# The C rows of a selective scan: a matmul from the small projection tile in place of a repeating transfer and a ScalarE copy

## The chip, the cores and the metric

The kernel runs on one core of a Trainium2 chip. The core has five engines with queues of their own: TensorE (PE in the profile; its weight loads are PEld), VectorE (DVE), ScalarE (ACT), GpSimd (POOL) and SyncE (SP), which here issues the DMA transfers; 16 DMA engines carry these. Each engine takes its instructions in the order of the program and waits for the others by semaphores. SBUF is the working memory of 128 partitions, PSUM the memory that TensorE writes, in banks of 512 fp32 numbers a partition.

The metric is the device time of one execution in microseconds (us), as the median over runs.

## What is computed

The program is a sequence of four layers on images of 4 x 64 x 64 positions and 128 channels. The first two hold a selective scan in four directions over the 4096 positions (`D` is 128 channels in layer 0 and 256 in layer 1, `N` is 16 states, the rank `R` is 4 and 8). Cut to what matters here:

```python
x_dbl = jnp.einsum('bkdl,kcd->bkcl', xs, x_proj_w)       # R + 16 + 16 rows a direction
dts, Bs, Cs = jnp.split(x_dbl, [R, R + N], axis=2)
dts = jnp.einsum('bkrl,kdr->bkdl', dts, dt_w)
delta = jax.nn.softplus(dts + dt_b[None, :, :, None])

def step(h, t):
    x_t, d_t, B_t, C_t = t
    h = jnp.exp(d_t[..., None] * A) * h + (d_t * x_t)[..., None] * B_t[:, :, None, :]
    return (h, jnp.einsum('bkdn,bkn->bkd', h, C_t))
```

Around the scans stand projections, small convolutions and normalisations; layers 2 and 3 (a message-passing layer and neighbourhood attention) follow after the scans.

## The kernel before

**Tiling.** A *task* is the scan of one image over 128 channels: 4 tasks in layer 0, 8 in layer 1 (two tiles of channels an image; the second task of such a pair has `t.first` set and uses the first one's projection again). A task has 16 *steps*: 4 directions times 4 stretches of `TS` = 1024 positions. A step has 16 *units* of 8 channels: the 128 partitions of a unit are 16 states times 8 channels. So there are 12 x 16 x 16 = 3072 units and 192 steps.

**One unit.** `load` (L429, SP's queue) brings `dub`, the product of delta and x for 8 channels, repeated for 16 states, from DRAM. `times_b` (L436, GpSimd) multiplies it by `repB`, the B rows, into `h`. `decay` puts delta, spread over the partitions, into PSUM by two bf16 matmuls (`da`, L444) and takes the exponent in place on ScalarE (L446). `scan` runs the recurrence on VectorE (L455), and after each odd unit multiplies the pair of `h` by C, `hc` (L465). `save` copies the last column of the pair as `state` (L476, ScalarE). `add_up` sums `hc` over the states by TensorE into `yps` (L536), `keep` (L546) and `sum_so_far` (L511, L519) carry the running sum. `h` has buffers for three pairs, `da` two, `dub` five.

**The order** is written out by hand in `Scans.run`: in slot u it issues the scan of u, the product with B of u + 3, C if u opens a step, the state of the last pair, the decay of u + 2, the summing of the last pair, then *pieces*: of the preparation of a later step, and of side work (the projections, convolutions and outputs of other images), and last the load of u + 6. A planner (`Plan`) keeps an account in us of how far TensorE, ScalarE and GpSimd are behind; `plan.slot` adds what a slot holds of fixed work (its two last arguments are TensorE's sums and ScalarE's copies) and a piece is let in when it fits. DMAs of the pieces are posted with a due time and issued in a later slot.

**The preparation** of a step (`prepare`) begins 22 units ahead of it. TensorE projects the 1024 positions in two halves of 512, side by side: rows 0 to R + 31 of the small tile `xd` hold delta's R rows, B's 16 and C's 16 of the first half, rows 64 on those of the second. ScalarE copies it from PSUM into `xd` (one buffer), and it is stored as `xdd` in DRAM (L348). The second task of a pair reads delta's R rows back (L356). From `xdd`, two transfers (L363) repeat each of the 16 rows of B and of C for 8 partitions into `repB` (two buffers) and `repC` (one buffer), 512 KB each. From `xd`'s first R rows, TensorE (`ms<-xd`), ScalarE and GpSimd make delta, its three bf16 parts and its product with x, which goes to DRAM (`dud`, L394) to be read as `dub`.

**C** is read by VectorE from PSUM: `bring_c`, at the first unit of a step, copies `repC` into the tile `C` (two banks, one buffer) on ScalarE (L482). It stands in ScalarE's queue behind the exponent of unit 1 and the pieces of the slot before, and ahead of the state copy, the exponent of unit 2 and the copy of `y`.

Operations that the planner counts all bear the line of its helper, L97.

Of the kernel before, what the change touches and what calls it, by code (L numbers as in the profile page):

```python
# [9 lines left out]
F32 = mybir.dt.float32  # L10
# [7 lines left out]
P = 128  # L18
H = 64
HW = 64  # L20
L = HW * HW
T = 512
NCH = L // T
ROWS = T // HW
NS = 16
ND = 4
NG = 16
TS = 1024
HALVES = TS // T
# [15 lines left out]
class Consts:  # L45


    def __init__(self, tc, pool, d_gather, d_spread):
        nc = tc.nc

        gather = pool.tile([P, 56], F32, name="gather")
        nc.sync.dma_start(out=gather, in_=d_gather)
        self.gather = [gather[:, 24 - 8 * jj : 56 - 8 * jj] for jj in range(4)]

        self.spread = pool.tile([96, 4, P], BF16, name="spread")
        with tc.tile_pool(name="spread32", bufs=1) as tmp:
            spread = tmp.tile([96, 4, P], F32, name="spread32")
            nc.sync.dma_start(out=spread, in_=d_spread)
            nc.vector.tensor_copy(self.spread, spread)
        self.ident = pool.tile([P, P], F32, name="ident")  # L60
        make_identity(nc, self.ident)
        self.ones128 = pool.tile([P, P], F32, name="ones128")
        nc.vector.memset(self.ones128, 1.0 / 128.0)
        self.cen128 = pool.tile([P, P], F32, name="cen128")
        nc.vector.tensor_sub(self.cen128, self.ident, self.ones128)
        self.cen256 = pool.tile([P, P], F32, name="cen256")
        self.neg256 = pool.tile([P, P], F32, name="neg256")
        nc.vector.memset(self.neg256, -1.0 / 256.0)
        nc.vector.tensor_add(self.cen256, self.ident, self.neg256)
        self.eps = pool.tile([P, 1], F32, name="eps")  # L70
        nc.vector.memset(self.eps, EPS)
# [34 lines left out]
UNIT = 3.6  # L106
# [7 lines left out]
class Plan:  # L114
# [22 lines left out]
    def post(self, chain, issue, due=0.0):  # L137

        if self.running:
            self.posted.append((chain, max(self.done, due), issue))  # L140
        else:
            issue()
# [77 lines left out]
class ScanWeights:  # L220


    def __init__(self, tc, pool, layer, d_xp, d_dtw, d_av):
        nc = tc.nc
        self.layer, self.nct, self.rank = layer, TILES[layer], RANKS[layer]
        nct, rank = self.nct, self.rank
        self.nc, self.pool, self.d_xp, self.d_dtw = nc, pool, d_xp, d_dtw
        n = ND * nct * NG
        av = pool.tile([P, n + 2 * ND * nct], F32, name=f"av{layer}")
        nc.sync.dma_start(out=av, in_=d_av)  # L230
        self.a = av[:, 0:n]
        nc.scalar.activation(self.a, self.a, AF.Exp)
        nc.vector.tensor_scalar_mul(self.a, self.a, -1.0)
        self.dtb = av[:, n : n + ND * nct].rearrange("p (k t) -> p k t", k=ND)
        ds = av[:, n + ND * nct :].rearrange("p (t k) -> p t k", t=nct)
        self.dsum = pool.tile([P, nct], F32, name=f"dsum{layer}")
        nc.vector.reduce_sum(self.dsum, ds, axis=AX.X)


    def load(self):  # L240

# [27 lines left out]
class Scans:  # L269
# [14 lines left out]
    @staticmethod  # L284
    def half(i):
        return slice(i * T, (i + 1) * T)
# [30 lines left out]
    def prepare(self, t, step):  # L317

        nc, W, half, post = self.plan, t.W, self.half, self.plan.post
        begin = self.plan.now  # L320
        k, c = t.steps[step]
        R = W.rank
        rows = R + 2 * NS
        if t.first is None:
            yield "PE" if W.nct > 1 else "PE ACT"

        xd = self.tile("xd", 1, shape=(P, T))
        if t.first is None:
            xdd = t.xdd[step] = self.dram.tile(
                [rows, TS], F32, name="xdd", tag=f"xdd{W.layer}", bufs=(4, 2 * len(t.steps))[W.layer]  # L330
            )
            ps = self.bank()
            for ti in range(W.nct):
                for i in range(HALVES):
                    nc.tensor.matmul(
                        image(ps[i * H : (i + 1) * H, :]),
                        W.xp[:, ti, k, :],
                        self.view(t.xc[ti], k, c, i, HALVES),
                        start=ti == 0,
                        stop=ti == W.nct - 1,  # L340
                    )
                if ti + 1 < W.nct:
                    yield "PE ACT" if ti + 2 == W.nct else "PE"
            nc.scalar.copy(xd, ps)

            def store_xd():
                for i in range(HALVES):
                    nc.sync.dma_start(out=xdd[:, half(i)], in_=xd[i * H : i * H + rows, :])  # L348

            post("prep", store_xd)  # L350
            ready = max(self.plan.done, self.plan.now) + LANDING
            yield "PE ACT"
        else:
            xdd, ready = t.first.xdd[step], begin
            for i in range(HALVES):
                nc.sync.dma_start(out=xd[i * H : i * H + R, :], in_=xdd[0:R, half(i)])  # L356
            yield "PE ACT", self.plan.now + LANDING
        out = t.prepared[step] = {}

        def repeat(i):  # L360
            rep = out["BC"[i]] = self.tile("rep" + "BC"[i], 2 - i)
            src = bass.AP(xdd.tensor, xdd.offset + (R + i * NS) * TS, [[TS, NS], [0, 8], [1, TS]])
            nc.sync.dma_start(out=rep, in_=src)  # L363

        for i, free in enumerate((5, 8)):
            post("rep", lambda i=i: repeat(i), max(begin + free * UNIT, ready))

        bias = W.dtb[:, k, t.ct : t.ct + 1]
        delta, low = self.tile("delta", 1), self.tile("low", 1)
        for i in range(HALVES):  # L370
            ps = self.bank()
            nc.tensor.matmul(
                ps,
                W.dtw[i * H : i * H + R, k, t.ct * P : (t.ct + 1) * P],
                xd[i * H : i * H + R, :],
                start=True,
                stop=True,
            )
            nc.scalar.activation(low[:, half(i)], ps, AF.Abs, bias=bias)
            nc.scalar.activation(delta[:, half(i)], ps, AF.Relu, bias=bias)  # L380
            yield "PE ACT" if i + 1 < HALVES else "ACT"
        nc.scalar.activation(low, low, AF.Exp, scale=-1.0)
        yield "ACT"
        nc.scalar.activation(low, low, AF.Ln, bias=1.0)
        yield "POOL"
        nc.gpsimd.tensor_add(delta, delta, low)
        yield "ACT POOL"
        parts = self.tile("parts", 1, shape=(P, 3, TS), dtype=BF16)
        nc.scalar.copy(parts[:, 0, :], delta)
        nc.gpsimd.tensor_mul(image(low), image(delta), self.view(t.xc[t.ct], k, c, 0, 1))  # L390
        yield "POOL"
        t.x_done = step == len(t.steps) - 1
        dud = out["du"] = self.dram.tile([P, TS], F32, name="dud", tag="dud", bufs=3)
        post("prep", lambda: nc.sync.dma_start(out=dud, in_=low))  # L394
        nc.gpsimd.tensor_sub(delta, delta, parts[:, 0, :])
        yield "ACT"
        nc.scalar.copy(parts[:, 1, :], delta)
        yield "POOL"
        nc.gpsimd.tensor_sub(parts[:, 2, :], delta, parts[:, 1, :])


        def own(part, j):
            if j == part == 0:
                out["delta"] = self.tile("dp", 2, shape=(96, 4, TS), dtype=BF16)
            nc.sync.dma_start(
                out=out["delta"][32 * part : 32 * part + 32, j, :], in_=parts[32 * j : 32 * j + 32, part, :]
            )

        for i in range(12):
            j, part = divmod(i, 3)  # L410
            post("rep", lambda part=part, j=j: own(part, j), begin + (9 + 0.7 * i) * UNIT)
        yield ""
# [65 lines left out]
    def bring_c(self, u):  # L478

        t, step, jj, j, g = self.unit(u)  # L480
        c = self.psum.tile([P, TS], F32, name="C", tag="C", bufs=1)
        self.nc.scalar.copy(c, t.prepared[step]["C"])  # L482
        t.prepared[step]["C"] = c

# [69 lines left out]
    def run(self, between):  # L556
# [10 lines left out]
        for u in range(-7, total):  # L567
# [14 lines left out]
            if u > 0 and u % 8 == 1:  # L582
                self.sum_so_far(u - 1)
            even, eighth, first_one = u % 2 == 0, u % 8 == 1, u % NG == 0
            self.plan.slot(
                u, 1.6 * even + 1.0 * eighth, 0.25 * even + 0.7 * (u % 8 == 0) + 1.1 * first_one
            )
            ahead, rest = divmod(u + AHEAD, NG)
            if rest == 0:
# [556 lines left out]
def scan_layers(tc, C, nb, x_in, d0, s0, d1, s1, out):  # L1146

    nc = tc.nc
    with ExitStack() as es:
# [1 line left out]
        side_pool = es.enter_context(tc.tile_pool(name="side", bufs=1))  # L1151
        psum = es.enter_context(tc.tile_pool(name="psum", bufs=1, space=PSUM))
        dram = es.enter_context(tc.tile_pool(name="dram", bufs=1, space=DRAM))
        Ws = [ScanWeights(tc, pool, i, *d) for i, d in enumerate((s0, s1))]
        plan = Plan(nc)
        side = Side(tc, C, side_pool, psum, dram, x_in, d0, d1, plan)
        side.x2 = out
# [876 lines left out]
```

## Time and profile before

| | us |
|---|---|
| median of 3 runs | 14127.82 (14112.14 to 14149.53) |
| the profiled execution, its time | 14143.9 |
| its span, first to last instruction | 14142.1 |
| scan stage, 195 to 11466 us | 11271 |
| VectorE busy in the scan stage | 10460.65 |
| GpSimd busy in the scan stage | 9272.69 |
| TensorE busy in the scan stage | 8107.24 |
| ScalarE busy in the scan stage | 6639.11 |
| mean granted TensorE clock in the scan stage | 0.70 |
| busy share of the 16 DMA engines there | 0.87, 213 GB/s |

The span's 40 equal slices show the stages: the scans fill the first 32, layers 2 and 3 the rest.

```profile
PE   5777777777766777677777777777777766657999
DVE  4998899989998999889998999999999945775666
ACT  3666566646665566556665555555555546554555
POOL 4777788768876888778887888888888843550000
DMA  6888889989898888989889888888888842442000
```

How to read the page: a group's line has the program line, the engine, the operation, the tile that is written and those that are read, the shapes and the count; then its busy time, the mean duration of one in ns, the idle time of the engine just before such instructions, and who ended most of it. In a list of waits a line has the engine and the tile that waited, whom it waited for, the sum in us, how many times, and the longest. In a timeline a line has start, length, engine, line and operation; neighbours of one kind are merged, and an fp32 matmul counts as two records.

### The profile page before, as it was taken

What the parts mean: (1) busy time and instruction counts of PE and PEld (TensorE: products, weight loads), DVE (VectorE), ACT (ScalarE), POOL (GpSimd) and SP (SyncE); (2) the same over time, 40 slices, a digit from 0 to 9 for tenths busy, and PEclk for the clock granted to TensorE, in tenths of its full rate; (3) what the DMA queues carried; (4) which work ended last, traced back from release to release, by engine and by line L of the source; (5) the groups of instructions that cost most, each with busy time, mean ns of one, the idle gap of its engine ahead of it and who ended that gap; (6) DMA issues with size and microseconds to landing.
All of it is one profiled execution on the core that took longest, in us unless ns stands there. A gap on an engine that the chain in (4) does not pass through costs nothing. (4 is left out here: it accounts for less than half of the span.)

```text
span 14142.1 us, 120207 instructions
## 1 busy us (share of the span) xinstructions
PE 10269.8 (73%) x36408; PEld 2614.3 (18%) x36408; DVE 12076.7 (85%) x6647; ACT 8107.1 (57%) x10782; POOL 9862.3 (70%) x4606
## 2 busy tenths in 40 slices
PE   5777777777766777677777777777777766657999
PEld 1111111111111111111111111111111111113555
DVE  4998899989998999889998999999999945775666
ACT  3666566646665566556665555555555546554555
POOL 4777788768876888778887888888888843550000
PEclk7766767767776767777766777767776678778999
DMA  6888889989898888989889888888888842442000
GB/s 163 218 217 220 206 216 226 219 212 217 219 232 202 213 214 213 224 208 218 219 217 223 217 204 202 204 202 222 205 208 202 196 111 65 104 109 59 13 14 8
DMA packets 900351, 2567.23 MB, mean 182 GB/s; under 512 B 145271, under 2 KB 166911, under 8 KB 891511
## 3 DMA queue, kind: packets, MB, share of 16 engines
q1 hardware_dynamic: 899703, 2559.53, 73.8%
q8 instruction: 291, 4.77, 0.2%
q14 instruction: 357, 2.92, 0.1%
HBM read 2135.67 MB, written 272.37 MB: 170 GB/s over the span
## 5 line engine op out<-in xcount | busy, mean ns | idle before, releaser
L436 POOL TENSOR_TENSOR h<-dub,repB 128x1024 f32<-128x1024 f32 x3072 | 7174.4, 2356 | 1326.2 <-DMA dub<-dud 947.5
L455 DVE TENSOR_TENSOR_SCAN h<-da,state,h 128x1024 f32<-128x1024 f32 x2304 | 5322.0, 2339 | 468.8 <-POOL h L436 267.4
L446 ACT ACTIVATE da<-da,av 128x1024 f32<-128x1024 f32 x3072 | 3339.4, 1088 | 2949.2 <-PE da L444 2938.4
L444 PE MATMUL da<-dp,spread 96*128 96x512 bf16 x6144 | 2533.8, 506 | 2516.6 <-DVE h L455 2459.6
L465 DVE TENSOR_TENSOR hc<-h,C 128x2048 f32<-128x2048 f32 x1536 | 3513.6, 2288 | 150.1 <-ACT C L482 92.0
L536 PE MATMUL yps<-hc,gather 128*32 128x512 f32 x12288 | 2473.7, 890 | 6.7 <-DVE hc L465 6.7
L455 DVE TENSOR_TENSOR_SCAN h<-da,h 128x1024 f32<-128x1024 f32 x768 | 1730.6, 2279 | 369.9 <-POOL h L436 266.3
L444 PEld LDWEIGHTS <-spread 96*128 96x128 bf16 x6144 | 565.4, 108 | 5811.1 <-issue 5664.3
L97 POOL TENSOR_TENSOR delta<-delta,low 128x1024 f32<-128x1024 f32 x192 | 451.8, 2353 | 593.5 <-ACT low L97 539.0
L97 PE MATMUL ms<-d,wts 128*128 128x512 f32 (+3 forms) x900 | 675.2, 876 | 198.7 <-POOL d L97 101.7
L97 ACT ACT_TABLE_LOAD x600 | 769.8, 1283 | 12.1 <-PE ms L97 1.7
L97 PE MATMUL ms<-xd,xpdt 8*128 8x512 f32 (+1 forms) x768 | 631.1, 913 | 127.2 <-ACT xd L97 34.9
L97 ACT CAST parts<-delta 128x1024 bf16<-128x1024 f32 x384 | 400.9, 1044 | 399.5 <-POOL delta L97 375.0
L519 PE MATMUL yps<-y,ident 128*128 128x512 f32 x576 | 515.1, 985 | 104.6 <-ACT y L546 104.0
L97 ACT ACTIVATE low<-ms,av 128x512 f32<-128x512 f32 x384 | 263.9, 687 | 525.2 <-PE ms L97 506.7
L1813 ACT ACTIVATE s<-s,nmax 128x512 f32<-128x512 f32 x512 | 366.1, 717 | 249.4 <-DVE nmax L1810 244.6
L97 POOL TENSOR_TENSOR low<-delta,xc 128x1024 f32<-128x1024 f32 x192 | 501.8, 2614 | 1.5
L97 PE MATMUL ms<-pad,diag 96*32 96x504 f32 (+1 forms) x2304 | 410.9, 818 | 94.0 <-DMA pad<-xid 48.2
L1441 ACT ACTIVATE hid<-hid,relb 128x1024 f32<-128x1024 f32 x288 | 322.7, 1146 | 262.9 <-DVE hid L1436 262.6
L536 PEld LDWEIGHTS yps<-hc,gather 128*32 128x32 f32 x12288 | 283.7, 128 | 1016.5 <-issue 1008.2
L1543 POOL TENSOR_TENSOR acc<-acc,part 128x1024 f32<-128x1024 f32 x120 | 311.2, 2599 | 215.7 <-DVE part L1537 160.3
L1802 PE MATMUL sps<-k,q 32*128 32x512 f32 x1024 | 444.4, 664 | 21.2 <-DVE s L1809 21.2
(276 smaller groups left out, 11290.2 us busy)
## 6 DMA issues: line engine op xcount, KB each, us to landing
dub<-dud SPq DMA_DIRECT2D x3072, 512.0 KB
dp<-parts SPq DMA_DIRECT2D x2304, 64.0 KB
repB<-xdd SPq DMA_DIRECT2D x192, 512.0 KB
repC<-xdd SPq DMA_DIRECT2D x192, 512.0 KB
dud<-low SPq DMA_DIRECT2D x192, 512.0 KB
spread<-gd SPq DMA_DIRECT2D x72, 1024.0 KB
pad<-xid SPq DMA_DIRECT2D x192, 256.0 KB
szd<-o SPq DMA_DIRECT2D x96, 256.0 KB
```

What stands on the lines that cost most here:

```text
L97: return call(*args, **kw)
L436: self.nc.gpsimd.tensor_mul(dbu, self.live.pop(("dub", u)), t.prepared[step]["B"])
L444: self.nc.tensor.matmul(da[:, cols], self.C.spread[:, jj, :], dp[:, j, cols], start=True, stop=True)
L446: self.nc.scalar.activation(da, da, AF.Exp, scale=t.W.a[:, at : at + 1])
L455: nc.vector.tensor_tensor_scan(h[:, way], da[:, way], h[:, way], 0.0 if step % NSTEP == 0 else t.states[step - 1][:, u % NG : u % NG + 1], ...
L465: nc.vector.tensor_mul(hc, pair, t.prepared[step]["C"].unsqueeze(1).to_broadcast([P, 2, TS]))
L519: self.nc.tensor.matmul(self.like_part(yps, k), self.C.ident, self.part(t.y, k, c, b), start=True, stop=False)
L536: self.nc.tensor.matmul(out, self.C.gather[jj], rhs, start=False, stop=jj == 3)
L1441: nc.scalar.activation(hid, hid, AF.Gelu, bias=self.relb[:, m, t : t + 1])
L1543: (nc.vector if alone and pair else nc.gpsimd).tensor_add(acc, acc, part)
L1802: nc.tensor.matmul(sps[:, h, :], q[ch, toks], k[ch, keys], start=True, stop=True)
L1813: nc.scalar.activation(s[:, i, :], s[:, i, :], AF.Exp, bias=nmax[:, h : h + 1], accum_out=total[:, h : h + 1],)
```

## The change

C no longer goes by way of `xdd` and `repC`. A selector `pick`, 128 x 128, is made at the start from the identity: column 8 n + i has a one in row R + 16 + n and another in row 64 + R + 16 + n. At the first unit of a step, two fp32 matmuls, one for each half of the positions, multiply `pick`'s rows by `xd`'s and so write C's 16 rows, each repeated for 8 partitions, into the two banks of `C`. For this `xd` is kept until then and has two buffers, and the second task of a pair reads all rows of `xdd` back. The transfer of `repC`, its tile and the copy L482 go. The planner's account of a step's first unit has 2.0 us more of TensorE and 1.1 us less of ScalarE.

```diff
@@ class ScanWeights, __init__ @@
+        self.pick = pool.tile([P, P], F32, name=f"pick{layer}")
+        one, two = (C.ident[:, i * H + rank + NS : i * H + rank + 2 * NS] for i in range(2))
+        both = [P, NS, P // NS]
+        nc.vector.tensor_add(
+            self.pick.rearrange("p (n i) -> p n i", n=NS),
+            one.unsqueeze(2).to_broadcast(both),
+            two.unsqueeze(2).to_broadcast(both),
+        )
@@ class Scans, prepare @@
-        xd = self.tile("xd", 1, shape=(P, T))
+        xd = self.tile("xd", 2, shape=(P, T))
...
-                nc.sync.dma_start(out=xd[i * H : i * H + R, :], in_=xdd[0:R, half(i)])
+                nc.sync.dma_start(out=xd[i * H : i * H + rows, :], in_=xdd[:, half(i)])
             yield "PE ACT", self.plan.now + LANDING
-        out = t.prepared[step] = {}
-
-        def repeat(i):
-            rep = out["BC"[i]] = self.tile("rep" + "BC"[i], 2 - i)
-            src = bass.AP(xdd.tensor, xdd.offset + (R + i * NS) * TS, [[TS, NS], [0, 8], [1, TS]])
-            nc.sync.dma_start(out=rep, in_=src)
-
-        for i, free in enumerate((5, 8)):
-            post("rep", lambda i=i: repeat(i), max(begin + free * UNIT, ready))
+        out = t.prepared[step] = {"xd": xd}
+
+        def repeat():
+            out["B"] = self.tile("repB", 2)
+            src = bass.AP(xdd.tensor, xdd.offset + R * TS, [[TS, NS], [0, 8], [1, TS]])
+            nc.sync.dma_start(out=out["B"], in_=src)
+
+        post("rep", repeat, max(begin + 5 * UNIT, ready))
@@ class Scans, bring_c @@
-        c = self.psum.tile([P, TS], F32, name="C", tag="C", bufs=1)
-        self.nc.scalar.copy(c, t.prepared[step]["C"])
-        t.prepared[step]["C"] = c
+        c = t.prepared[step]["C"] = self.psum.tile([P, TS], F32, name="C", tag="C", bufs=1)
+        rows = t.W.rank + 2 * NS
+        for i in range(HALVES):
+            at = slice(i * H, i * H + rows)
+            self.nc.tensor.matmul(
+                c[:, self.half(i)], t.W.pick[at, :], t.prepared[step]["xd"][at, :], start=True, stop=True
+            )
@@ class Scans, run @@
             self.plan.slot(
-                u, 1.6 * even + 1.0 * eighth, 0.25 * even + 0.7 * (u % 8 == 0) + 1.1 * first_one
+                u, 1.6 * even + 1.0 * eighth + 2.0 * first_one, 0.25 * even + 0.7 * (u % 8 == 0)
             )
```

More of the change, by code (lines that the diff above doesn't have):

```diff
@@ L220, with __init__ @@
 class ScanWeights:
-    def __init__(self, tc, pool, layer, d_xp, d_dtw, d_av):
+    def __init__(self, tc, C, pool, layer, d_xp, d_dtw, d_av):
         nc = tc.nc
@@ L1153, in scan_layers @@
         dram = es.enter_context(tc.tile_pool(name="dram", bufs=1, space=DRAM))
-        Ws = [ScanWeights(tc, pool, i, *d) for i, d in enumerate((s0, s1))]
+        Ws = [ScanWeights(tc, C, pool, i, *d) for i, d in enumerate((s0, s1))]
         plan = Plan(nc)
```

## The prediction

> **What bounds the kernel now.** I read the page's head and busy shares first, then the costliest groups, then the waits of VectorE in the scan stage (195 to 11466 us), then the timeline of one step's start.
>
> ```profile
> span 14142.1 us, 120207 instructions
> PE 10269.8 (73%) x36408; PEld 2614.3 (18%) x36408; DVE 12076.7 (85%) x6647; ACT 8107.1 (57%) x10782; POOL 9862.3 (70%) x4606
> L436 POOL TENSOR_TENSOR h<-dub,repB 128x1024 f32<-128x1024 f32 x3072 | 7174.4, 2356 | 1326.2 <-DMA dub<-dud 947.5
> L455 DVE TENSOR_TENSOR_SCAN h<-da,state,h 128x1024 f32<-128x1024 f32 x2304 | 5322.0, 2339 | 468.8 <-POOL h L436 267.4
> L465 DVE TENSOR_TENSOR hc<-h,C 128x2048 f32<-128x2048 f32 x1536 | 3513.6, 2288 | 150.1 <-ACT C L482 92.0
> ```
>
> The scan stage is four fifths of the span, and VectorE fills it: 5322.0 + 1730.6 (the scans without a state) + 3513.6 = 10566 us, of which 10461 lie in these 11271 us. So the change can win there at most the 810 us in which VectorE stands. Its waits say for whom:
>
> ```profile
> DVE h L455 <- POOL h L436: 533.7, 175, 183.6
> DVE h L455 <- ACT da L446: 259.9, 281, 11.7
> DVE hc L465 <- ACT C L482: 92.0, 81, 3.2
> ```
>
> The 183.6 is the kernel's start, so GpSimd costs 350 us in the stage, the decay on ScalarE 260, and C 92 (in 81 of 192 steps). The first two belong mostly to other work; the third is what is edited.
>
> Why C is late, at the start of one step (start, length, engine; unit 0's scan begins at 7947.54):
>
> ```profile
> 7947.54 4.74 DVE L455 TENSOR_TENSOR_SCAN h<-da,state,h 128x1024 f32<-128x1024 f32 x2
> 7947.96 0.60 PE L444 MATMUL da<-dp,spread 96*128 96x512 bf16 x2
> 7949.94 0.59 PE L444 MATMUL da<-dp,spread 96*128 96x512 bf16 x2 [1.38 <-DVE h L455]
> ...
> 7953.06 1.28 ACT L97 ACT_TABLE_LOAD   x1
> ...
> 7954.36 1.02 ACT L482 COPY C<-repC 128x1024 f32<-128x1024 f32 x1
> 7955.31 0.19 ACT L476 COPY state<-h 128x2 f32<-128x2 f32 x1
> 7955.41 1.08 ACT L446 ACTIVATE da<-da,av 128x1024 f32<-128x1024 f32 x1
> 7955.41 2.29 DVE L465 TENSOR_TENSOR hc<-h,C 128x2048 f32<-128x2048 f32 x1 [3.13 <-ACT C L482]
> ```
>
> C's bank is free and repC has landed; the copy stands in ScalarE's queue behind side work (GELU and two table loads). TensorE meanwhile waits 1.38 us for scan 0 before the decay of unit 2, just where the changed kernel puts its matmuls.
>
> **The change, part by part.** All sums are made against the profiled execution (14143.9 us); the median of the runs shown is 16.1 us below it, and I take that off at the end.
>
> *1. C by TensorE in place of the copy.* The price comes from the preparation's own fp32 matmul of 512 columns, two records each, and from four query-key matmuls on rows 32 to 63 and 64 to 95:
>
> ```profile
> 9022.65 1.12 PE L97 MATMUL ms<-xd,xpdt 8*128 8x512 f32 x2
> 4478.02 2.07 PE L97 MATMUL ms<-xd,xpdt 8*128 8x512 f32 x2
> 13080.28 1.12 PE L1802 MATMUL sps<-k,q 32*128 32x512 f32 x2
> 13081.69 1.13 PE L1802 MATMUL sps<-k,q 32*128 32x512 f32 x4
> ```
>
> One matmul is 1.12 us at full clock and 2.07 at half; two on different rows into different banks take the time of one (1.13 against 1.12). C's halves read rows 0 to 39 and 64 to 103 (layer 0: to 35 and 99) and write two banks, so 1.12 to 2.07 for both, unless they run in turn (a rival). The granted clock was half at 104 of 191 step starts, so I take 1.6.
>
> I laid that price over each of the 191 step starts of the trace: C begins when both TensorE's last matmul ahead of unit 2's decay and the old C's last reader have ended; hc starts when VectorE and C are ready; the exponent of unit 2 moves up into the place of the copy, behind the 0.19 us state copy, but not before its decay; scan 2 starts after hc, exponent and h. In the step shown C would run from 7948.6 to 7949.7, hc at 7952.3 to 7954.6, the exponent from 7954.55 to 7955.63, and scan 2 would start there instead of at 7957.61: 1.95 us won of the 3.13 waited. TensorE comes a median 1.46 us late to that place, yet C is done before scan 1 ends in most steps: what is left of C's wait is 14 us at 1.12 and 48 at 2.07. Scan 2 starts earlier by 94 us in sum at the one price and 60 at the other; 76 at 1.6. Of these 76, 16 lie in steps where VectorE next waits for GpSimd's h before GpSimd itself waits for VectorE or ScalarE: lost there. Term: -60, bounds -94 and -44 (60 less 16).
>
> The Trainium skill speaks against it: TensorEngine Tiling, "Tiling Modes", says that a change of tiling mode drains TensorE, and C adds two changes a step. The trace shows a second decay matmul 0.38 us after the first, and the four-column gather 0.56 us after it, so 0.18 a change; with that C costs 2.4 at half clock, and the term would be about -26 in place of -44.
>
> *2. 192 x 1.016 = 195 us leave ScalarE*, all at the step's start, where it is 84 to 87% busy (units 0 and 1) against 50 to 70% elsewhere. VectorE waited for decays of units 2 to 5 for 75 us (0.0, 13.8, 21.3, 39.8); the 69.5 at unit 1 stand ahead of the copy and stay. Bounds 0 and -75; a third is taken, since ScalarE is behind by more than one copy there: -25.
>
> *3. The repC transfer, 192 x 512 KB = 96 MB, 3.9% of 2567 MB,* and its place in SP's queue, where it waited for C's buffer 230 us in all with the dub loads behind it. In the 15 us after repC's issue GpSimd waited only 99 us for dub in all 192 steps, where an even spread of 947.5 over the stage gives 242: it collides with little. Bounds 0 and -37 (99 of 947.5 of VectorE's 350); I take 3.9% of 350, rounded to -15. The wider xd load (64 steps, two of 80 KB in place of 16) adds no instruction; 8.4 MB at the stage's 213 GB/s are 39 us if nothing hid them. The planner puts its first use 10 us later, and VectorE's queued scans cover it: 0, upper bound +39.
>
> *4. xd in two buffers, pick, the start.* Preparation of step s+1 starts six units before C of step s is read; the buffer it takes was last read a step ago: no wait. Pick is one small VectorE addition per layer (0.3 us, as the 128x128 ones): 0.
>
> *5. The planner* is told of 2.0 us of TensorE and no more of 1.1 us of ScalarE in unit 0. In the built program side and preparation matmuls behind unit 2's decay fall from 196 to 19, so C and these change places; the 177 go to the other units. VectorE waited 79 us for decays that came late because TensorE was busy with such matmuls. Bounds 0 and +79; by 177 of 3092 moved, some three times as dear where they crowd: +15.
>
> Sum: -60 - 25 - 15 + 15 = -85, so 14059 for such an execution and **14043** against the median. Bounds: -44 + 79 + 39 = +74 at worst; -94 - 75 - 37 = -206 at best.
>
> **Rivals.**
>
> *A. Hidden anyway.* GpSimd is 88 to 98% busy from unit 1 to 11, and VectorE waits for it 175 times, nearly once a step; what is won at the step's start is stood out a few units later. For: those shares. Against: GpSimd waits 267 us for state copies, that is, for VectorE's pace, and in 60 of the 76 us this comes first. Time: -15, 14113.
>
> *B. TensorE becomes the wait.* C stands ahead of unit 2's decay, the gather of the last pair and unit 3's decay in one queue. If the halves run in turn at half clock, C takes 4.15 us; laid over the step starts this makes scan 2 later by 96 us, hc by 101. The turning point is 3.1 us. With -25 from part 2 that is +71: 14199. For: TensorE is already 80 to 92% busy in odd units. Against: the 1.13 row.
>
> *C. DMA is the true pace.* The 16 engines are 87% busy in the stage; 3.9% off could shorten all of dub's latency. If GpSimd's lateness halves, -175 replaces -15: -245, 13883. Against: the 99 us above.
>
> *D. It doesn't do it:* the matmuls wait for something that the copy didn't (xd's load), and time is as before, 14128.
>
> **How the numbers follow.** Forecast 0.54, A 0.16, B 0.14, C 0.13, D 0.03. Three runs lie within 37 us, so 0.3% (42 us) is what can be told from no change: faster means under 14085. That holds for the forecast and C: 0.67; A and D: 0.19; B: 0.14. The forecast's own range is its bounds without the worst xd load, 13922 to 14163; with most of C below and without B's far side I give 13880 to 14150.
>
> **What would show it.** No repC issues and no L482 copy; VectorE's wait for C (now on TensorE) 14 to 48 us in place of 92; C's four records in 1.2 to 2.1 us, two starting within 10 ns; ScalarE busy 195 us less; waits for the decay below 260 and for h near 350; DMA bytes in the stage down by 90 MB. It would be wrong if C's records run one after another (B), if the decay's waits rise by more than C's fall (part 5), or if the waits for h grow by what C's lose (A).

## The result and the profile after

The changed kernel takes 14102.4 us (median of 13 runs, 14086.6 to 14121.9) against 14133.2 (13 runs beside it, 14112.1 to 14159.5): a ratio of 0.9975, 95% interval 0.9967 to 0.9982. By the ratio that is 35 us won, where 85 were forecast. Its profiled execution spans 14107.7 us.

The lines of the page that answer to those shown before:

```profile
span 14107.7 us, 121017 instructions
PE 10457.0 (74%) x37176; PEld 2664.9 (19%) x37176; DVE 12083.0 (86%) x6649; ACT 7942.8 (56%) x10590; POOL 9871.3 (70%) x4606
L443 POOL TENSOR_TENSOR h<-dub,repB 128x1024 f32<-128x1024 f32 x3072 | 7180.9, 2358 | 1301.9 <-DMA dub<-dud 971.2
L462 DVE TENSOR_TENSOR_SCAN h<-da,state,h 128x1024 f32<-128x1024 f32 x2304 | 5325.3, 2340 | 493.4 <-ACT da L453 228.4
L472 DVE TENSOR_TENSOR hc<-h,C 128x2048 f32<-128x2048 f32 x1536 | 3514.0, 2288 | 115.8 <-PE C L492 42.4
```

The engines did what the edit says: ScalarE is busy 164 us less, TensorE 187 us more (768 more records), and nothing changed for VectorE's work. What VectorE waits for in the scan stage (engine and tile, whom for, sum in us, times, longest):

```profile
DVE h L462 <- POOL h L443: 468.0, 143, 183.6
DVE h L462 <- ACT da L453: 304.4, 305, 14.8
DVE h L462 <- ACT state L483: 60.2, 63, 6.2
DVE hc L472 <- PE C L492: 42.4, 36, 4.2
DVE hc L472 <- remote: 11.6, 5, 3.8
```

C's own wait fell from 92.0 to 54.0 us (the "remote" row is also a product that stood for C, with no releaser found). The wait for GpSimd, less the 183.6 of the start, fell from 350.1 to 284.4, which I had put at -15. But decays rose from 259.9 to 304.4 and states from 36.2 to 60.2, where a fall was forecast. The four together fell by 35 us, as the time did. The line for the states before, which answers to the third above:

```profile
DVE h L455 <- ACT state L476: 36.2, 36, 2.8
```

The place where C comes late now, in the timeline of one step (start, length; weight loads, DMA issues and what stands at the three dots are left out):

```profile
3113.97 4.66 DVE L462 TENSOR_TENSOR_SCAN h<-da,state,h 128x1024 f32<-128x1024 f32 x2
3114.37 0.61 PE L451 MATMUL da<-dp,spread 96*128 96x512 bf16 x2
...
3115.12 1.12 PE L97 MATMUL ms<-xd,xpdt 4*128 4x512 f32 x2
3116.28 0.69 ACT L97 ACTIVATE low<-ms,av 128x512 f32<-128x512 f32 x1 [0.18 <-PE ms L97]
3116.87 0.68 ACT L97 ACTIVATE delta<-ms,av 128x512 f32<-128x512 f32 x1
3117.60 1.97 PE L97 MATMUL ms<-d,wts 64*64 64x512 f32 x4 [1.36 <-ACT delta L97]
3119.50 2.08 PE L492 MATMUL C<-xd,pick 36*128 36x512 f32 x4
...
3121.51 1.04 PE L451 MATMUL da<-dp,spread 96*128 96x512 bf16 x2
3121.63 2.29 DVE L472 TENSOR_TENSOR hc<-h,C 128x2048 f32<-128x2048 f32 x1 [3.00 <-PE C L492]
```

C could have started soon after 3114, when the last product ended and its banks came free. It stands behind two pieces of the slot before it, a preparation matmul and a side matmul. The second needs the bank `ms`, which ScalarE empties with two activations first: 1.36 us in which TensorE stands still with C behind it. So C was taken out of ScalarE's queue and is still late by ScalarE's work, through the shared bank. Behind C, the decay of unit 2 begins at 3121.51 instead of with the end of scan 0, near 3116.3.

### The profile page after: what moved, and what is told of

Same layout as the page of the kernel before. It is cut to its first block, busy times and chain, and to the rows that moved or that the text cites. A ratio compares the mean times of both kernels' runs of the same rounds, so it can differ in the third digit from the quotient of the medians.

```text
span 14107.7 us, 121017 instructions
## 1 busy us (share of the span) xinstructions
PE 10457.0 (74%) x37176; PEld 2664.9 (19%) x37176; DVE 12083.0 (86%) x6649; ACT 7942.8 (56%) x10590; POOL 9871.3 (70%) x4606
## 5 line engine op out<-in xcount | busy, mean ns | idle before, releaser
L547 PE MATMUL yps<-hc,gather 128*32 128x512 f32 x12288 | 2436.1, 877 | 5.6 <-DVE hc L472 5.6
L1447 DVE TENSOR_TENSOR hid<-cen,near 128x1024 f32<-128x1024 f32 x288 | 336.1, 1214 | 111.2 <-PE cen L1440 111.1
```

The costliest lines, as they stand in the source:

```text
L547: self.nc.tensor.matmul(out, self.C.gather[jj], rhs, start=False, stop=jj == 3)
L1447: nc.vector.tensor_add(hid.rearrange("p i (r w) -> p (i r) w", w=HW), cen[pair].rearrange("p i (r w) -> p (i r) w", w=HW), self.near[m][s] ...
```

## The experiments

Each kernel was timed in 5 to 11 runs, with runs of the kernel before among them. The waits are VectorE's in the scan stage, in us, from one profiled execution each; h is without the kernel's start (182.5 to 184.8). That execution took 23 us more than the median in e1, 19 in e5 and 16 in e8, and lay within 11 of it elsewhere, so a few us between two rows mean nothing. "C" holds the waits for C and the rows without a releaser.

| run | ratio to before (95%) | h | decay | state | C |
|---|---|---|---|---|---|
| before | 1 | 350 | 260 | 36 | 92 |
| the change | 0.9975 (0.9967 to 0.9982) | 284 | 304 | 60 | 54 |
| e1 change, old account | 0.9962 (0.9948 to 0.9976) | 310 | 294 | 44 | 30 |
| e2 before, new account | 1.0021 (1.0012 to 1.0029) | 353 | 290 | 38 | 92 |
| e3 before, no transfer | 0.9963 (0.9950 to 0.9975) | 282 | 268 | 33 | 92 |
| e4 change, ScalarE kept busy | 0.9983 (0.9974 to 0.9992) | 285 | 298 | 49 | 48 |
| e5 e1 with C nearly free | 0.9943 (0.9929 to 0.9956) | 302 | 300 | 40 | 1 |
| e6 e1 with C twice | 1.0014 (1.0005 to 1.0023) | 280 | 307 | 49 | 100 |
| e7 e1, C behind the decay | 1.0012 (1.0003 to 1.0021) | 289 | 319 | 43 | 104 |
| e8 before, small transfer | 0.9971 (0.9961 to 0.9980) | 284 | 273 | 41 | 93 |
| e9 e1, copy out of the account | 0.9963 (0.9950 to 0.9975) | 314 | 289 | 38 | 41 |
| e10 e1, TensorE in the account | 0.9963 (0.9951 to 0.9976) | 313 | 247 | 57 | 64 |
| e11 e1, C ahead of the pieces | 0.9945 (0.9933 to 0.9958) | 279 | 315 | 40 | 0 |
| e12 e1, room ahead of C | 0.9977 (0.9968 to 0.9986) | 272 | 348 | 44 | 39 |

In what follows a ratio is turned into us by 14133; one interval reaches 11 to 20 us to either side, that of a difference of two runs up to 28.

### The planner's account alone: e1 and e2

```diff
-                u, 1.6 * even + 1.0 * eighth + 2.0 * first_one, 0.25 * even + 0.7 * (u % 8 == 0)
+                u, 1.6 * even + 1.0 * eighth, 0.25 * even + 0.7 * (u % 8 == 0) + 1.1 * first_one
```

e1 makes this edit to the changed kernel, e2 the reverse one to the kernel before.

> The changed kernel with the planner's account of the kernel before (no 2.0 us of TensorE, again 1.1 us of ScalarE in a step's first unit). Theory A, the new account moves side work to where decays and state copies come late: VectorE's waits fall back from 304 to about 260 us for decays and from 60 to about 36 for states, and the time is 40 to 70 us under the changed kernel's, 14030 to 14060. Theory B, the added matmuls on TensorE do it whatever the account: the waits for decays stay at 300 or above, and the time is that of the changed kernel (14102) or up to 40 us above.

> The kernel before with the changed kernel's account alone (C still by transfer and ScalarE copy). Theory A: VectorE's waits for decays and states rise by about 70 us, time about 14170 to 14200. Theory B: they stay within 20 us of 260 and 36, time within 25 us of 14133.

e1 is 54 us under the kernel before, 18 more than the change; e2 is 30 us above it. The new account costs something on its own: e2 is clear of noise, while the 18 us have 22 to either side. Theory A has the sign, at half its size. Theory B holds for the rest: with the old account decays are still at 294.

Waits of e1, decays and C, and then of e2, h and decays (the same columns as above):

```profile
DVE h L462 <- ACT da L453: 294.4, 310, 16.3
DVE hc L472 <- PE C L492: 29.0, 29, 4.2
```

```profile
DVE h L455 <- POOL h L436: 535.8, 174, 182.8
DVE h L455 <- ACT da L446: 290.4, 275, 16.5
```

In e2 nothing moved but the decays, 30 us up, and that is its time. Of VectorE's waits for a decay, those in which TensorE came late from other matmuls, nearly all of pieces, are some 80 us before and 103 in e2; the rest, 180 and 184 us, stand behind other work of ScalarE.

### The transfer alone: e3 and e8

e3 takes the transfer away, lets the copy read `repB`, and changes nothing else:

```diff
-        for i, free in enumerate((5, 8)):
-            post("rep", lambda i=i: repeat(i), max(begin + free * UNIT, ready))
+        post("rep", lambda: repeat(0), max(begin + 5 * UNIT, ready))
...
-        self.nc.scalar.copy(c, t.prepared[step]["C"])
+        self.nc.scalar.copy(c, t.prepared[step]["B"])
```

> The kernel before without the transfer of repC; ScalarE copies the B tile into C's bank instead, so the output uses B for C. All else as before. Theory A, the 96 MB are what GpSimd's waits gained: VectorE's waits for h fall from 350 us in the scan stage to about 285, time about 14070. Theory B, they collide with nothing, as the 99 us in the 15 us behind their issue said: h within 25 us of 350, time 14115 to 14133.

e8 keeps it with its place and its waits and cuts its bytes:

```diff
+            later = i and hasattr(self, "rep_c")
-            rep = out["BC"[i]] = self.tile("rep" + "BC"[i], 2 - i)
+            rep = out["BC"[i]] = self.rep_c if later else self.tile("rep" + "BC"[i], 2 - i)
...
+            if i:
+                self.rep_c = rep
+            if later:
+                n = TS // 16
+                rep, src = rep[:, 0:n], bass.AP(src.tensor, src.offset, [[TS, NS], [0, 8], [1, n]])
```

> The kernel before, where the transfer of repC brings only 64 of 1024 columns after the first time (32 KB instead of 512 KB), into one kept tile and with the same waits and places in SP's queue; the other columns are those of the first step. Theory A, the bytes are what counts: h falls to about 285 as without the transfer, time about 14080. Theory B, its place and wait in SP's queue count: h stays at 350, time 14120 to 14133.

e3 wins 52 us, e8 41: theory A in both. So the bytes of the transfer are worth more than the whole change won; its place and its wait in SP's queue were worth nothing that these runs tell apart. In every trace without the full transfer VectorE waits 272 to 314 us for h, in the two with it (before and e2) 350 and 353. GpSimd's products with B in e3, and VectorE's waits:

```profile
L435 POOL TENSOR_TENSOR h<-dub,repB 128x1024 f32<-128x1024 f32 x3072 | 7174.5, 2356 | 1253.4 <-DMA dub<-dud 881.9 <-ACT state L475 278.4 <-DVE h L454 23.9
DVE h L454 <- POOL h L435: 466.2, 153, 184.5
DVE h L454 <- ACT da L445: 267.6, 294, 9.1
DVE hc L464 <- ACT C L481: 91.5, 81, 3.1
```

GpSimd's wait for dub fell by 66 us (947.5 to 881.9) and VectorE's wait for h by 68 (350 to 282). By unit, 51 of the 66 lie at units 8 to 11, which waited 107 us before and 55 in e3. GpSimd is 2 to 4 us ahead of VectorE there, and VectorE's waits for h at these units fell from 74 to 38 us. That the two sums fell alike is in part chance: at unit 0 GpSimd waits 314 us for dub before and 327 in e3, and VectorE for h 57 and 41. In the changed kernel, too, GpSimd's waits at units 8 to 11 fell, to 49, though their sum rose to 971 by 56 us more at unit 0, where VectorE's wait for h stayed (57 and 61).

These are the loads that stand behind the transfer in SP's queue: in 137 of 192 steps the next load issued after it is that of unit 8, and the product of that next load starts 16 us after the transfer's issue in the median. e8 issues the transfer at the same places, so the two traces can be laid side by side. GpSimd's waits for the first four loads behind it fell from 153 to 96 us. Its waits within 15 us of the issue did not fall (99 us before, 110 in e8); 96 of those 99 us are for loads that were issued before the transfer.

### What C's wait and C's work are worth: e5 and e6

```diff
+        if step:
+            t.prepared[step]["C"] = t.prepared[0]["C"]
+            return
```

> The changed kernel with the old account (e1), and C's matmuls only at the first step of each task, so 12 times instead of 192; the other steps multiply by that first step's C. No wait for C and no work for it. Theory A, TensorE's added work makes decays, states and h late in e1: the waits return to those of the kernel without the transfer (decays 268, h 282, states 33) with none for C, time 14075 less 60 to 90, about 13985 to 14015. Theory B, what C's wait wins is stood out later whatever TensorE does: decays and h stay at e1's 294 and 309, time 14045 to 14075.

```diff
-        for i in range(HALVES):
+        for i in (0, 1, 0, 1):
```

> e1 with C's two matmuls issued twice a step (1.1 to 2.1 us more of TensorE ahead of unit 2's decay). Theory A: decays, h and C's wait rise by 60 to 90 us in sum, time about 14140 to 14165. Theory B: 14075 to 14095.

e5 has neither transfer nor copy, nearly no matmul for C and no wait for it. Its waits:

```profile
DVE h L462 <- POOL h L443: 485.3, 171, 183.6
DVE h L462 <- ACT da L453: 300.0, 317, 12.1
DVE h L462 <- ACT state L483: 40.1, 45, 3.0
```

Against e3, the same without the transfer but with the copy, 91 us of waiting for C are gone, and the time is only 28 us lower. Decays rose by 32, h by 20, states by 7: 59 of the 91 are stood out a little later, with nearly no work added on TensorE. By the times it is 91 less 28, so 63, with 26 to either side. That is what theory B said, though the time, 14041, fell between the two expectations. The work of C then costs 27 us (e1 over e5, with 28 to either side; VectorE waits 30 for it in e1), and a second pair of matmuls 74 more (e6 over e1), nearly all of it as wait for C, from 30 to 100. So theory A holds for TensorE's time (e6, clear of noise), theory B for the wait removed.

### C's place in the queue: e7 and e11

e7 moves the call of `bring_c` behind that of `decay(u + 2)`; e11 moves it one slot up:

```diff
-            if u >= 0 and u % NG == 0:
-                self.bring_c(u)
...
                 self.add_up(u // 2 - 1)
+            if 0 <= u + 1 < total and (u + 1) % NG == 0:
+                self.bring_c(u + 1)
```

> e1 with C's matmuls behind unit 2's decay in TensorE's queue instead of ahead of it. If C's place ahead of the decay delays it, the waits for decays of units 2 to 5 fall from 109 us to about 80 and C's wait rises from 30 to 60 or more: time within 15 of e1's 14074. If the place is nothing, only C's wait rises: 14090 to 14110.

> e1 with C's matmuls one slot earlier in TensorE's queue, behind unit 1's decay and ahead of the side and preparation matmuls of that slot, which so wait for the last pair's product. C's own time was worth 33 us (e1 against e5). If what made C late is those matmuls ahead of it, C's wait falls from 30 to under 10 and the time to 14045 to 14065; if the matmuls that now stand behind C make the decays late instead, decays rise by 20 or more and the time is 14075 or above.

Behind the decay, C waits for scan 0 too and VectorE for C: 104 us, and decays did not fall but rose to 319. The place ahead of the decay was no loss; e7 came out worse than both expectations (14148). Ahead of the pieces, no product waits for C at all. Decays rise from 294 to 315, so both halves of that expectation came true, and the time is lower: 78 us under the kernel before, level with e5, where C costs nearly nothing. Against e1 that is 24 us, within the 27 that noise can make. Its decays:

```profile
DVE h L462 <- ACT da L453: 315.3, 348, 15.4
```

### ScalarE's relief, and the account once more: e4, e9, e10, e12

e4 is the changed kernel with two casts of 512 columns a step on ScalarE that nobody reads.

```diff
+        idle = self.tile("idle", 1, shape=(P, T), dtype=BF16)
+        for i in range(HALVES):
+            self.nc.scalar.copy(idle, t.prepared[step]["B"][:, self.half(i)])
```

> The changed kernel, with ScalarE still busy as long as the copy at a step's first unit: two casts of 512 columns of the B tile into an unused tile (about 1.1 us), which nobody waits for. Theory A, ScalarE's relief is worth about 25 us as predicted: time about 14125, waits for decays up by about 25. Theory B, it is worth nothing: 14102 within 12. Theory C, it is worth far more, hidden by a loss elsewhere: 14150 or above.

That puts 206 us of busy time back on ScalarE. Theory B fits best: the median is 1.4 us under the change's 14102, and decays did not rise (298 against 304). By the ratios e4 is 11 us above the change, with 17 to either side, so the relief is worth between nothing and 28 us, and theory A's 25 is not quite shut out.

> e1 with the account of ScalarE's copy taken out and none of TensorE put in (half of the new account). If the missing 1.1 us of ScalarE make the new account dear, the time is that of the changed kernel, about 14100, with decays at 300 or above and states near 60; if the 2.0 us of TensorE do, it is e1's 14074 within 12.

> e1 with the 2.0 us of TensorE put in and the 1.1 us of ScalarE kept (the other half). If the 2.0 us of TensorE make it dear: about 14100; if ScalarE's do: 14074 within 12.

> e1 with 1.0 us of TensorE entered in the account of the slot ahead of C (the last unit of a step), so that fewer matmuls stand ahead of C. If room there is what C needs: C's wait under 15 and 14050 to 14065; if the matmuls that go elsewhere cost as much as in the new account: 14080 to 14105.

Both halves of the account alone give e1's ratio, so which of them makes the whole dear stays open, as does whether they only do it together: the intervals (0.9950 to 0.9976) reach those of the change. e12 moved the room to the slot ahead of C, and C's wait did not fall (39, against 30 in e1), while decays rose to 348 (14101 us, as the second half of its expectation had it): what is kept out of one slot comes late in another.

## Why the prediction was wrong

The direction was right, and the size was not: 35 us for 85. That the direction held is luck: it rests on the transfer, forecast at -15; without its 52 us the other parts come to +17. The runs split the change into the transfer (-52, e3), C's wait and the copy on ScalarE taken away (-28, e5 against e3), C's work on TensorE (+27, e1 against e5) and the account (+18, change against e1). The sum, -35, is the measured one by construction; the four have 18, 26, 28 and 22 us to either side.

**Part 1 failed: "-60, bounds -94 and -44".** Measured, -1 (-28 + 27; e1 against e3, which also holds parts 2 and 4 and the wider xd load), with 27 us to either side, so beyond its own bounds. The price of C was right: 1.13 to 2.08 us in nearly all steps, 1.62 in the mean, for the 1.6 taken; the halves started 6 or 7 ns apart and ran side by side, and rival B's 4.15 never came. In wait for C, too, the old account's 30 us lie between the 14 and 48 given; the new account's 54 lie above. The step that failed is *"Of these 76, 16 lie in steps where VectorE next waits for GpSimd's h before GpSimd itself waits for VectorE or ScalarE: lost there."* I counted as lost only what GpSimd would take, and as kept all that a late decay or state would take. e5 shows the price: of the 91 us removed 59 came back, 20 as waits for h, near the 16 counted, and 39 as waits for decays and states, which I had put at nothing. The trace before had a sign of it: of its 260 us of waits for decays, 80 stand behind other matmuls of TensorE and 180 behind other work of ScalarE. That such work does not wait for VectorE, and so is late however early VectorE comes, is argued and not shown step by step. Rival A, "hidden anyway", had the right mechanism for two thirds of what was removed, with too narrow a cause.

**Part 2, "-25", can't be told from nothing:** 11 us with 17 to either side (e4). The waits for decays of units 2 to 5, of which a third was to go, were 75 us before, 71 in the change and 77 in e4. The largest share of them stands right behind the preparation's activation of delta, 29 us before and 34 in the change, and not the copy.

**Part 3, "-15, bounds 0 and -37", measured -52 (e3) and -41 (e8),** outside its bounds. Two steps were wrong. The first is the window: *"In the 15 us after repC's issue GpSimd waited only 99 us for dub in all 192 steps"*. The 99 us are there, but 96 of them are for loads that were issued before the transfer, and without its bytes they did not fall (110 in e8). What fell were the waits for the loads behind it, used 16 us after the issue and later. The second is the conversion, *"99 of 947.5 of VectorE's 350"*: it let VectorE feel a third of every GpSimd wait. But at unit 0, where GpSimd has a lead of 5.6 us in the median, 314 us of its waits left VectorE 57; at units 8 to 11, with 2 to 4 us, 107 left 74. Rival C had this mechanism at about three times its size (-175).

**Part 4** was right: none of C's matmuls waits for `xd`'s load, and no copy for its buffer. What the wider xd load of part 3 cost, no run tells apart. **Part 5**, +15, was 18 on the change, with 22 to either side, and 30 on the kernel before (e2, with 12).

**The rule that spoke against the change,** from the Trainium skill, TensorEngine Tiling, "Tiling Modes" (a change of tiling mode drains TensorE), agrees with the trace of the changed kernel. A decay that follows a full-array matmul starts 0.43 us after the start of its last record at full clock and 0.85 at half; one that follows C, 0.52 and 0.99. That is 0.09 to 0.14 a change where I took 0.18. If the change before C costs as much, it is 35 to 54 us of TensorE's time in all steps; by the prediction's own slope (94 us at 1.12, 60 at 2.07) an estimate of 6 to 10 us of the kernel's, a small part of the miss.

**A better version** is e11: the change with the old account and C's matmuls ahead of the pieces, at 0.9945 (0.9933 to 0.9958) against the change's 0.9975 (0.9967 to 0.9982). Its gain over the change is clear of noise, that over e1 is not.

## What to carry to other kernels

A wait that is removed from the bounding engine pays only as far as the next thing that is late for a reason of its own; list those, whoever they wait for, before counting the wait as won. A transfer is priced at the loads that stand behind it, when they are used, and most where their user has little lead over the bounding engine; not at the moment of its issue, and not by a share of the mean. And an instruction moved to another queue inherits what stands ahead of it there: with C past those pieces (e11) the ratio is 0.9945, beside 0.9943 with C nearly free (e5).

## What was not expected of the hardware

Taking 1/26 of the traffic off DMA engines that are 87% busy (213 GB/s) won 52 us, or 0.37%, with no transfer ever being the named releaser of VectorE in the scan stage; with 64 of 1024 columns left in each row the gain was about the same (41 us, h at 284), and the number of packets was the same (900351), so it is the bytes and not the 128 rows or the issue that counted most here. The duration of a single 4 KB packet hardly changed by it (median 274 ns in the trace of before, 273 in that of e3).

The granted TensorE clock rose with C's matmuls: in the median of the runs it was 0.735 to 0.737 before and 0.735 in e3, 0.742 in the change, 0.745 in e1 and 0.753 in e6. In the profiled executions C's records take 311 us, but TensorE is busy only 187 us longer, since its other work took 94 us less (10176 for 10270). So what C's work cost (e1, e6) is net of a higher clock; how much of the time that clock gave back, no run shows. The gain of e3 came without it.
